# Cross-attention with a second attention branch on one core: attended values as one piece, the transposes of y as a stage of their own, and a least amount of fill for each step

## The chip, the cores and the metric

The kernel runs on one core of one Trainium2 chip. The metric is the device time of one execution in microseconds (us), here the median of several runs. The core has a matrix engine (TensorE, "PE"; its loads of stationary operands are listed apart as "PEld"), VectorE ("DVE"), ScalarE ("ACT") and GpSimd ("POOL"); SyncE ("SP") issues most of the transfers. Every engine works through its own list of instructions in the listed order, and semaphores join the lists. Matrix products are accumulated in PSUM, a memory of eight banks, and must be copied or reduced out of it by another engine before the bank can be used again.

## What is computed

The inputs are x, 2 x 2048 x 640 numbers in float32, a context of 2 x 128 x 384, and weights. The context's first 124 tokens are text tokens; its last 4 form a second branch. There are 8 heads of 80.

```python
query = hidden_states @ Wq
keyt = enc @ Wk
valt = enc @ Wv
hs = _mha(query, keyt, valt)                        # softmax over 124 keys
ca_q1 = jnp.einsum('btc,th->bch', ca, Wq_ca)        # 384 distinct rows
ca_q1 = ca_q1[:, indices, :]                        # spread over 2048 rows
ca_hs1 = _mha(ca_q1, residual, residual)            # keys and values are x itself
ca_q2 = ca_hs1 @ Wq
ca_hs2 = _mha(ca_q2, ca @ Wk_ca, ca @ Wv_ca)        # softmax over 4 keys
out = (hs + ca_hs2) @ Wout + b_out + residual
```

Since the 2048 queries of the second branch are only 384 distinct rows, that branch is computed for 384 rows and its part of the output is added to the row tiles by an indirect transfer.

## The kernel before

The 2 x 2048 rows of x are cut into 32 row tiles of 128 rows, two of which make a *unit* (16 units, m = 0 to 15), and into 8 *blocks* of 512 rows (b, sb). Two streams of work share TensorE.

**The second branch** is the main line, once per batch b. `yz_block` (L712) multiplies a block of x, transposed, with a small matrix (tiles `pyz`), ScalarE copies the result out and adds ones (L731, tile `yz`), and TensorE turns it by eight transposes (tiles `pt_y`) which are copied into `y_sb`. `maxima` (L743) computes scores `s1`, 4 matmuls of a small tile shape at a time into four banks, and VectorE takes their maxima (`mx`, 2.3 us each). `less_maxima` (L762) subtracts them. `contraction` (L776) computes the scores again the other way round (`s2`), ScalarE takes the exponential of them (`ea`, L807), and TensorE accumulates `acc` from `ea` and `y_sb`; at its end stand a transpose (`pt_acc`), small operations on VectorE (`prod`, `s2f`, `p2`), a transpose (`pt_p2`) and three products (`po2`) whose result `o2` is written to DRAM.

**The text branch** is the fill. For a unit m it consists of `queries` (tiles `pq`, five matmuls each), `scores` (L918: two `sc` tiles of three matmuls per row tile; VectorE takes the maximum `m` and subtracts it, ScalarE takes the exponential in one instruction for both), `divided` (L955: VectorE sums, `r`, and GpSimd multiplies, L962), `turned` (L965: VectorE transposes both row tiles into `eb`, one transfer writes them to DRAM as `kept`, and after `wait` further steps four transfers read them back as `pT`), and `values` (L994: three tiles `ph` of attended values, the first two of four matmuls, the third of eight with a smaller shape, each copied to `hsT`; then four tiles `po` of five matmuls for the output projection, each added to the row tile `xo` by VectorE). Row tiles that are finished before `o2` exists are written to a buffer in DRAM (`early`) and are read back (`xe`) and completed later.

**What sets the order.** All matmuls are kept in the order in which the program emits them. `TensorInOrder` (L20) adds up a planned time `pe.us` for them. `weave(main, fill)` (L1106) runs the main line step by step; each step yields a gap in planned microseconds, and `fill.run` then emits pieces of the fill until the gap is used. A piece ends where the fill's generator yields; it may overshoot the gap, and the debt, a negative `due`, is carried to the next steps, which then may get no piece at all. `Mix` (L133) takes pieces in turn from its fills: `own` (what the main line needs next: loads, transposes of x, `yz` blocks), `text` and `later`. Each part is a `Stage` with needs: names in `done` or conditions. `x_turn` (L694) needs 24 planned us after its load. `Mix.until` (L159) forces parts through up to a named one. `ahead(m)` (L1120) makes unit m's stage: `together` (L1074) runs `turned(m + 1)`, `residual(m + 1)`, `completed`, the queries and scores of unit m + 2 and `values(m)` in turn, one piece of each at a time. So between two `ph` tiles of unit m stands a piece of each of the others, a score tile `sc` for instance.

PSUM: three banks (`ps_m`), to which a fourth (`ps_a`) is added in the second batch's maxima, serve the tiles of the fill and the small ones of the main line; four banks hold `s1` or `s2`. From the end of the second contraction on, eight banks serve the fill. `evacuate` (L268) copies a tile out on VectorE in the first contraction, on ScalarE in the second batch's maxima, on both in turn in the second contraction and the tail.

The phases by the trace of before: setup to 58 us, maxima of batch 0 to 169, contraction 0 from 171 to 312, maxima of batch 1 to 482, contraction 1 from 484 to 625, the tail (units 10 to 15, without a main line) to the end.

The functions that the change touches, and what calls them:

Of the kernel before, what the change touches and what calls it, by code (L numbers as in the profile page):

```python
# [19 lines left out]
class TensorInOrder:  # L20
# [3 lines left out]
    def __init__(self, tc):  # L24
        self.tc, self.us = tc, 0.0
# [107 lines left out]
class Mix:  # L133

    def __init__(self, pe, *fills):
        self.pe, self.fills, self.at = pe, [[f, w, f.us] for f, w in fills], None

# [19 lines left out]
    def until(self, done, what):  # L159
        while what not in done:  # L160
            for f, _, _ in self.fills:
                if any(getattr(p, "what", None) == what for p in f.parts):
                    while self.at is not None and self.at is not f and self.at.open:
                        self.at.step(self.pe)
                    self.at = f
                    if not f.step(self.pe):
                        assert what in done or self.step(), what
                    break
            else:
                assert what in done, what  # L170
# [3 lines left out]
def kernel(  # L174
# [40 lines left out]
    pe = TensorInOrder(tc)  # L215
# [8 lines left out]
    NSB = S // 512  # L224
# [15 lines left out]
    done = set()  # L240
    slots = Slots(done, xqp, NSB + 1)
# [400 lines left out]
    blocks = [(b, sb) for b in range(B) for sb in range(NSB)]  # L642
    yz_of, o2_of, q_of, e_of, pT_of, xr_of, early_of = {}, {}, {}, {}, {}, {}, {}
    whole = set()
    coming = []

    def x_tile(b, sb, again):

        users = [] if again else [("yz", b, sb)]
        users += [("q", b, sb)] if again or b == 0 else []  # L650
        t = slots.tile([P, 4, NCH, P], f"xt_{b}_{sb}", users)
        for kind in ("q",) if again else ("q", "yz") if b == 0 else ("yz",):
            xt[kind, b, sb] = t
        return t
# [57 lines left out]
    def yz_block(b, sb):  # L712


        t = xt["yz", b, sb]
        yz = yz_of[b, sb] = cap.tile([P, 2, 512], F32, tag="yz", name=f"yz_{b}_{sb}", bufs=NSB + 1)
        ps = [mm_tile(f"pyz_{b}_{sb}_{u}") for u in range(2)]
        for c in range(4):
            half = slice(2 * G * (c % 2), 2 * G * (c % 2 + 1))
            matmul(  # L720
                ps[c // 2][half, :], wyz[:, b, c, :, :].rearrange("p j k -> p (j k)"), t[:, :, c, :],
                start=True, stop=False, skip_group_check=True,
            )
        for u in range(2):
            half = slice(2 * R * u, 2 * R * (u + 1))
            matmul(
                ps[u], wyz4[half, b, :, :].rearrange("p g k -> p (g k)"), t[half, :, 4, :],
                start=False, stop=True, skip_group_check=True,
            )
        for u in range(2):  # L730
            nc.scalar.activation(yz[:, u, :], ps[u], AF.Identity, bias=ones)  # L731
        yield
        for u in range(2):
            py = mm_tile(f"pt_y_{b}_{sb}_{u}")
            for k in range(4):
                transpose(py[:, k * P : (k + 1) * P], yz[:, u, k * P : (k + 1) * P], ident)
            evacuate(
                y_sb[:, 4 * sb : 4 * sb + 4, 4 * u : 4 * u + 4, :].rearrange("p s g k -> p s (g k)"),
                py.rearrange("p (s k) -> p s k", s=4),
            )  # L740
            yield
# [220 lines left out]
        nc.gpsimd.tensor_tensor(et, et, r.unsqueeze(2).to_broadcast([P, HEADS, NK]), ALU.mult)  # L962
        e_of[b, st] = e

    def turned(m, wait=3):  # L965


        eb = pools["eb"].tile([P, 4, 2, HEADS, R], F32, tag="eb", name=f"eb_{m}")
        for k, at in enumerate(tiles(m)):
            last = dve.last  # L970
            ins = dve.transpose(eb[:, :, k], e_of.pop(at).rearrange("p h (j b) -> p j h b", j=4))
            dve.behind(ins, last)
        kept = hbm.tile([P, 4, 2 * HEADS * R], F32, tag="hbm", name=f"kept_{m}")
        dma(kept, eb.rearrange("p j k h a -> p j (k h a)"))
        for _ in range(wait):
            yield
        pT = pT_of[m] = pools["pT"].tile([P, 4, 2, HEADS, R], F32, tag="pT", name=f"pT_{m}")
        by_keys = kept.rearrange("(i b) j n -> j b i n", i=4)
        for j in range(4):
            dma(pT[R * j : R * (j + 1)].rearrange("p i k h a -> p i (k h a)"), by_keys[j])  # L980
        yield
# [12 lines left out]
    def values(m):  # L994

        N = 2 * P
        b = tiles(m)[0][0]
        xr = xr_of.pop(m)
        pT = pT_of.pop(m)
        hsT = []  # L1000
        for c0, n in ((0, 2), (2, 2), (4, 1)):
            ph = mm_tile(f"ph_{m}_{c0}")
            for k in range(n):
                for h in (2 * (c0 + k), 2 * (c0 + k) + 1) if c0 < 4 else ():
                    half = slice(VH * (h % 2), VH * (h % 2 + 1))
                    matmul(
                        ph[half, k * N : (k + 1) * N], vpad[b][:, h, :VH], pT[:, :, :, h, :].rearrange("p i k a -> p k i a"),
                        start=True, stop=True, skip_group_check=True,
                    )
            for h in (0, 2, 4, 6, 1, 3, 5, 7) if c0 == 4 else ():  # L1010
                quarter = slice(R * (h // 2), R * (h // 2 + 1))
                matmul(
                    ph[quarter, :N], vpad[b][:, h, VH:], pT[:, :, :, h, :].rearrange("p i k a -> p k i a"),
                    start=(h % 2 == 0), stop=(h % 2 == 1), skip_group_check=True,
                )
            t = pools["ht"].tile([P, n * N], F32, tag=f"ht{n}", name=f"hsT_{m}_{c0}", bufs=2)
            evacuate(t, ph[:, : n * N])
            hsT += [t[:, k * N : (k + 1) * N] for k in range(n)]
            yield
        for k, (b, st) in enumerate(tiles(m)):  # L1020
            rows = slice(k * P, (k + 1) * P)
            for u in range(2):
                cols = slice(u * HALF, (u + 1) * HALF)
                po = mm_tile(f"po_{b}_{st}_{u}")
                for c in range(NCH):
                    matmul(
                        po[:, :HALF], hsT[c][:, rows], wout_sb[:, c, cols],
                        start=(c == 0), stop=(c == NCH - 1),
                    )
                    if c == 2:  # L1030
                        yield WITHIN
                dve.tensor_tensor(xr[k][:, cols], xr[k][:, cols], po[:, :HALF], ALU.add)
                yield
            if ("o2", b) in done:
                if m not in whole:
                    add_second(xr[k], b, st)
                dma(out[b, st * P : (st + 1) * P, :], xr[k])
            else:
                early_of[b, st] = hbm.tile([P, H], F32, tag="early", name=f"early_{b}_{st}", bufs=8)
                dma(early_of[b, st], xr[k])  # L1040
# [30 lines left out]
    def stage(what, gen, *needs):  # L1071
        return Stage(done, what, gen, *needs)
# [32 lines left out]

    def weave(main, fill):  # L1106

        due = 0.0
        for gap in main:
            due = fill.run(due + gap)  # L1110

    mx_of = {}
    sq_stack = ExitStack()
# [32 lines left out]
    def rows_stages(b, sb, *needs, again=False):  # L1146
        return [
            stage(("load", b, sb), x_load(b, sb, again), lambda: not coming, *needs),
            stage(
                ("again" if again else "x", b, sb), x_turn(),  # L1150
                lambda: not coming or pe.us > coming[0] + 24.0,
            ),
        ]

    def yz_stage(b, sb, *needs):
        return stage(("yz", b, sb), yz_block(b, sb), *needs)

    def early(n):
        needs = [("x", *blocks[n])] if n else []
# [3 lines left out]
    own = Fill(  # L1163
        done,
        loads[0][0],
        stage("keys", setup_keys()),
        loads[0][1],
        loads[1][0],
        yz_stage(0, 1, ("half", 0, 0)),
        loads[1][1],  # L1170
        loads[2][0],
        stage("values", setup_values()),
        yz_stage(0, 2, ("half", 0, 1)),
        loads[2][1],
        yz_stage(0, 3, ("half", 0, 2)),
    )
    text = Fill(done, *[early(n) for n in range(NSB)])
    Mix(pe, (text, 1)).run(12.5)
    fill = Mix(pe, (own, 1), (text, 1))
    weave(setup_a2(), fill)  # L1180
    own.parts.insert(0, yz_stage(0, 0))
    for sb in range(NSB):
        fill.until(done, ("yz", 0, sb))
        weave(maxima(0, sq, mx_of[0], sb, 2.4), fill)
# [12 lines left out]
        own.add(*rows_stages(1, sb, slots.free(1)))  # L1197
    later = Fill(done, *rows_stages(1, 0, slots.free(1), ("x", 1, 1), again=True))
    for sb in range(2, NSB):
        later.add(*rows_stages(1, sb, slots.free(1), ("yz", 1, 0)))  # L1200
    for sb in range(1, NSB):
        later.add(*rows_stages(1, sb, slots.free(1), ("room", NSB + sb - 1), again=True))
    fill = Mix(pe, (own, 1), (text, 1), (later, 1))
# [4 lines left out]
    on[0] = "A"  # L1208
    ps_turns[:] = [ps_m, ps_m, ps_m, ps_a]
    own.add(  # L1210
        yz_stage(1, 0),
        *[yz_stage(1, sb, ("half", 1, sb - 1), ("x", 1, sb)) for sb in range(1, NSB)],
    )
    for sb in range(NSB):
        fill.until(done, ("yz", 1, sb))
# [42 lines left out]
```

## Time and profile before

| | |
|---|---|
| median of 9 runs | 771.64 us (769.08 to 773.0) |
| profiled execution | 770.01 us, of which the span from first to last instruction is 768.3 |
| granted TensorE clock, mean | 0.998 |
| busy in the span: PE, PEld | 740.6 us, 378.9 us |
| busy in the span: DVE, ACT, POOL | 374.5 us, 195.1 us, 134.3 us |
| most costly groups on PE: po, pq (both weights), sc, s (both ways), acc, ph | 187.4, 188.0, 95.4, 114.1, 54.6, 51.1 us |

The profile gives for each engine the time in which it was busy, in the order of its groups of instructions ("out<-in", with the shapes) and the idle time just before them with the engine that ended it ("<-DVE hsT" means that the copy into hsT came last). The timeline lists instructions by start (us) and duration (us), neighbours of one kind joined into one row with "xN"; in brackets stands the idle time ahead of it. A matmul on 32-bit data is listed as two records, so a tile of three matmuls is "x6". In the text a distance is taken from start to start, which includes what a matmul's neighbours cost it.

### The profile page before, as it was taken

The page shows a single profiled execution, that of the slowest core. Times are in us where ns is not written, and L with a number is a line of the kernel's source. Part 1 is how long each engine was busy: PE and PEld are TensorE (multiplying, and loading weights), DVE is VectorE, ACT ScalarE, POOL GpSimd, SP SyncE. Part 2 cuts the span into 40 slices and gives each one's busy share as a digit, 9 for nine tenths or more (in the row PEclk, how much of TensorE's full clock was granted, in tenths as well). Part 3 has the DMA queues.
Part 4 walks back from the last instruction along what each step waited for, and adds up shares of the span by engine and source line. Part 5 has one row for each costly group of instructions (what it writes and reads, how often), then busy time and mean ns, then how long its engine had stood idle before and what let it go on. Part 6 is the DMA issues. An engine that isn't in the chain of part 4 may idle for free.

```text
span 768.3 us, 9354 instructions
## 1 busy us (share of the span) xinstructions
PE 740.6 (96%) x3785; PEld 378.9 (49%) x3785; DVE 374.5 (49%) x502; ACT 195.1 (25%) x241; POOL 134.3 (17%) x192
## 2 busy tenths in 40 slices
PE   7999999999998999989999999999999999999997
PEld 4653343343344445555545454444533556556664
DVE  2134753563365345578758586421530626346631
ACT  2212121104335433231111110443534321011100
POOL 7000000000111012217221221010010022432320
PEclk9999999999999999999999999999999999999999
DMA  9704540000476664499997267320920427785873
GB/s 287 164 0 69 71 85 0 1 0 1 131 124 139 155 121 130 131 236 197 266 185 209 52 151 130 110 52 18 181 67 1 150 71 222 163 219 168 215 216 90
DMA packets 146853, 95.63 MB, mean 124 GB/s; under 512 B 118069, under 2 KB 118389, under 8 KB 144762
## 3 DMA queue, kind: packets, MB, share of 16 engines
q1 hardware_dynamic: 141690, 84.44, 44.2%
q0 software_dynamic: 5120, 10.59, 8.0%
q8 instruction: 30, 0.49, 0.3%
q14 instruction: 13, 0.11, 0.0%
HBM read 63.48 MB, written 31.52 MB: 124 GB/s over the span
## 4 chain that ended last, share of the span: by engine, by line
PE 87%; DVE 6%; DMA 2%; ACT 2%; issue 2%; POOL 0%; SPq 0%; DVEq 0%; ACTq 0%; POOLq 0%
PE po L28 22%; PE pq L28 22%; PE s L28 13%; PE sc L28 10%; PE acc L28 6%; PE ph L28 5%; PE pyz L28 3%; DVE m L55 1%; DVE p L55 1%; PE pk L28 1%; ACT ea L807 1%; PE pt_y L41 1%; DVE mx L55 1%; PE pv L28 1%; DMA pT<-kept 1%
## 5 line engine op out<-in xcount | busy, mean ns | idle before, releaser
L28 PE MATMUL po<-wout_sb,hsT 128*128 128x320 f32 x640 | 187.4, 438 | 0.9 <-DVE xo L55 0.6
L28 PEld LDWEIGHTS po<-wout_sb,hsT 128*128 128x128 f32 x640 | 118.3, 190 | 72.0 <-issue 28.2
L55 DVE TENSOR_REDUCE mx<-s 128x4 f32<-128x2048 f32 x48 | 109.9, 2289 | 83.0 <-PE s L28 83.0
L28 PE MATMUL pq<-xt,wq_sb 128*128 128x512 f32 x320 | 150.2, 605 | 0.0
L807 ACT ACTIVATE ea<-s 128x1536 f32<-128x1536 f32 x64 | 92.7, 1448 | 105.2 <-PE s L28 105.1
L55 DVE TENSOR_TENSOR xo<-xo,po 128x320 f32<-128x320 f32 x64 | 31.0, 484 | 152.7 <-PE po L28 152.7
L962 POOL TENSOR_TENSOR p<-p,r 128x992 f32<-128x992 f32 x32 | 63.6, 2030 | 231.2 <-DVE r L55 221.6
L28 PE MATMUL sc<-kpad,q 128*128 128x248 f32 x384 | 95.4, 385 | 2.2 <-DVE p L55 1.6
L28 PEld LDWEIGHTS pq<-xt,wq_sb 128*128 128x128 f32 x320 | 57.4, 189 | 79.4 <-issue 74.7
L28 PEld LDWEIGHTS sc<-kpad,q 128*128 128x128 f32 x384 | 68.8, 189 | 32.9 <-issue 19.4
L28 PE MATMUL s<-ca,yz 32*128 32x384 f32 x512 | 59.4, 533 | 4.5 <-ACT ea L807 4.1
L268 ACT COPY q<-pq 128x512 f32<-128x512 f32 x30 | 17.6, 585 | 164.1 <-PE pq L28 164.1
L55 DVE TENSOR_REDUCE m<-sc 128x4 f32<-128x496 f32 x64 | 42.3, 663 | 34.0 <-PE sc L28 34.0
L28 PE MATMUL s<-yz,ca 32*128 32x512 f32 x384 | 54.7, 640 | 3.2 <-DVE mx L55 3.2
L1044 POOL DMA_INDIRECT xo<-o,query x25 | 39.2, 1569 | 92.3 <-DVE xo L55 23.7
L28 PE MATMUL acc<-ea,y_sb 128*32 128x384 f32 x512 | 54.6, 498 | 0.0
L28 PE MATMUL ph<-pT,vpad 128*32 128x256 f32 (+1 forms) x512 | 51.1, 387 | 2.2 <-DMA pT<-kept 1.9
L947 ACT ACTIVATE p<-p 128x992 f32<-128x992 f32 x32 | 33.0, 1031 | 74.2 <-DVE p L55 74.0
L55 DVE TENSOR_TENSOR p<-sc,m 128x496 f32<-128x496 f32 x64 | 42.7, 669 | 1.6
L268 ACT COPY hsT<-ph 128x512 f32<-128x512 f32 (+1 forms) x25 | 12.9, 515 | 106.3 <-PE ph L28 106.2
L55 DVE STREAM_TRANSPOSE eb<-p 128x1024 f32<-128x1024 f32 x32 | 38.0, 1222 | 2.2 <-POOL p L962 2.2
L55 DVE TENSOR_REDUCE r<-p 128x8 f32<-128x992 f32 (+1 forms) x34 | 37.9, 1115 | 0.0
(136 smaller groups left out, 435.8 us busy)
## 6 DMA issues: line engine op xcount, KB each, us to landing
kept<-eb SPq DMA_DIRECT2D x16, 1024.0 KB, 4.8
pT<-kept SPq DMA_DIRECT2D x64, 256.0 KB, 5.1
xi<-in_x_dram SPq DMA_DIRECT2D x44, 256.0 KB, 6.4
xo<-in_x_dram SPq DMA_DIRECT2D x32, 320.0 KB, 5.1
out_dram<-xo SPq DMA_DIRECT2D x25, 320.0 KB, 2.7
xi<-in_x_dram SPq DMA_DIRECT2D x44, 64.0 KB, 5.2
early<-xo SPq DMA_DIRECT2D x7, 320.0 KB, 2.2
xe<-early SPq DMA_DIRECT2D x7, 320.0 KB, 5.1
```

The source lines that it names most:

```text
L28: ins = self.tc.nc.tensor.matmul(out, lhsT, rhs, **kw)
L41: ins = self.tc.nc.tensor.transpose(out, in_, ident)
L55: self.last = getattr(self.tc.nc.vector, name)(*args, **kw).ins
L268: nc.scalar.copy(dst, src)
L807: nc.scalar.activation(e, q4[:, :, :CAD], AF.Exp, scale=SCALE)
L947: nc.scalar.activation(e[:, :, :NK], e[:, :, :NK], AF.Exp, scale=SCALE)
L962: nc.gpsimd.tensor_tensor(et, et, r.unsqueeze(2).to_broadcast([P, HEADS, NK]), ALU.mult)
L1044: nc.gpsimd.indirect_dma_start(out=t, out_offset=None, in_=o2_of[b], in_offset=bass.IndirectOffsetOnAxis(ap=query[:, st : st + 1], axis=0) ...
```

## The change

1. `values`: the `yield` behind each of the three `ph` tiles becomes a single one behind all three. The sixteen matmuls of a unit's attended values are one piece.
2. `turned`: the transfers of `pT` are issued after two further steps instead of three.
3. The `yz` stage becomes two: `yzT` (the matmuls `pyz` and ScalarE's copies) and `yz` (the transposes `pt_y` and their copies), which needs a planned time of 1.0 us since the first. The slot of the transposed x is free, and later loads may start, with `yzT`.
4. `weave`: what a step may fill is at least 0.5 planned us (or the step's own gap, where that is less), whatever the debt. So each step with a gap gets at least one piece.
5. `Mix.until` sets `Mix.hurry` where nothing else is left to step; two conditions on planned time are then passed over.

```diff
@@ class Mix
+    hurry = False
@@ Mix.until
-                    if not f.step(self.pe):
-                        assert what in done or self.step(), what
+                    if not f.step(self.pe) and what not in done and not self.step():
+                        Mix.hurry = True
+                        assert f.step(self.pe), what
+                        Mix.hurry = False
@@ x_tile
-        users = [] if again else [("yz", b, sb)]
+        users = [] if again else [("yzT", b, sb)]
@@ yz_block
             nc.scalar.activation(yz[:, u, :], ps[u], AF.Identity, bias=ones)
+        yz_at[b, sb] = pe.us
         yield
+
+    def y_rows(b, sb):
+
+        yz = yz_of[b, sb]
         for u in range(2):
             py = mm_tile(f"pt_y_{b}_{sb}_{u}")
@@ turned
-    def turned(m, wait=3):
+    def turned(m, wait=2):
@@ values
             hsT += [t[:, k * N : (k + 1) * N] for k in range(n)]
-            yield
+        yield
@@ weave
-            due = fill.run(due + gap)
+            due = fill.run(max(due + gap, min(gap, 0.5)))
@@ rows_stages
-                lambda: not coming or pe.us > coming[0] + 24.0,
+                lambda: Mix.hurry or not coming or pe.us > coming[0] + 24.0,
@@ yz_stage
-    def yz_stage(b, sb, *needs):
-        return stage(("yz", b, sb), yz_block(b, sb), *needs)
+    def yz_stages(b, sb, *needs):
+        return [
+            stage(("yzT", b, sb), yz_block(b, sb), *needs),
+            stage(("yz", b, sb), y_rows(b, sb), lambda: Mix.hurry or pe.us > yz_at[b, sb] + 1.0),
+        ]
@@ the loads of later blocks
-        later.add(*rows_stages(1, sb, slots.free(1), ("yz", 1, 0)))
+        later.add(*rows_stages(1, sb, slots.free(1), ("yzT", 1, 0)))
```

The calls of `yz_stage` become calls of `yz_stages`, whose two parts stand one behind the other in the same places. The transposes and matmuls, their shapes and their numbers are those of before. In the order that results, the three `ph` tiles of a unit are adjacent in all sixteen units (before, in units 14 and 15), ten row tiles go through `early` instead of seven, and in one tile of queries and one of attended values ScalarE and VectorE exchange their parts as copiers.

## The prediction

> **What bounds the kernel now.** I read the page first, then TensorE's waits, then stretches of the timeline, then the clock by windows.
>
> ```profile
> PE 740.6 (96%) x3785; PEld 378.9 (49%) x3785; DVE 374.5 (49%) x502; ACT 195.1 (25%) x241; POOL 134.3 (17%) x192
> PE 87%; DVE 6%; DMA 2%; ACT 2%; issue 2%; POOL 0%; SPq 0%; DVEq 0%; ACTq 0%; POOLq 0%
> ```
>
> TensorE (PE) is busy for 96% of the span and is 87% of the chain that ended last. The change issues the same matmuls in another order, so it can only save in two places: in TensorE's waits, and in what a matmul costs after a neighbour of another shape. The waits by releaser (us in total, times, longest):
>
> ```profile
> PE s L28 <- ACT ea L807: 4.1, 5, 1.8
> PE s L28 <- DVE mx L55: 3.2, 3, 1.4
> PE pt_y L41 <- ACT yz L731: 3.1, 4, 0.8
> PE ph L28 <- DMA pT<-kept: 1.9, 1, 1.9
> PE sc L28 <- DVE p L55: 1.6, 1, 1.6
> ```
>
> These five are 13.9 us. The timeline of unit 0 in contraction 0 shows how such a wait arises:
>
> ```profile
> 222.60 3.65 POOL L962 TENSOR_TENSOR p<-p,r 128x992 f32<-128x992 f32 x2 [21.60 <-DVE r L55]
> 226.28 1.25 DVE L55 STREAM_TRANSPOSE eb<-p 128x1024 f32<-128x1024 f32 x1 [0.56 <-POOL p L962]
> 227.44 0.64 DVE L55 TENSOR_REDUCE m<-sc 128x4 f32<-128x496 f32 x1
> 228.00 0.68 DVE L55 COPY hsT<-ph 128x512 f32<-128x512 f32 x1
> 228.74 1.08 PE L28 MATMUL ph<-pT,vpad 128*64 128x256 f32 x8 [0.23 <-DVE hsT L55]
> 233.07 0.93 PE L28 MATMUL s<-ca,yz 32*128 32x384 f32 x8 [1.79 <-ACT ea L807]
> ```
>
> VectorE works in order: it waits for GpSimd's product, transposes it (eb), and only then reduces scores that stood ready since 222.7 and copies out ph_0_0. TensorE meanwhile had other work, 6.05 us between ph_0_0 (222.69) and ph_0_2 (228.74), so it paid 0.23. That other work is what the change takes from between the ph tiles.
>
> **The change, part by part.** The sum is made against the profiled execution: 770.01 us, of which 768.3 span. The median of the nine runs, 771.64, lies 1.63 above it; I add a difference to the median.
>
> *Order alone.* The program's counts of matmuls are equal. (a) Three ph tiles with other work between them cost 1.01 each (ph at 222.69, next matmul 223.70); the one group that before already has together (750.36 to the po at 753.24) costs 2.88. 14 of 16 units are split before: 14 x (3.04 - 2.88) = 2.1 to 2.2 saved. (b) Two sc tiles between small-tile matmuls cost 2.70 together (216.89 to 219.59), one alone 1.46 (213.79 to 215.25): a pair of switches between full-array and small-tile matmuls is 0.22, about 0.1 each. The order after has 29 switches fewer (259 to 230): 2.8. (c) acc followed directly by a ph of the last chunk is cheaper by 0.11 than elsewhere; four such places go: +0.45; pt_y beside other neighbours +0.15. Sum -4.3.
>
> *Waits that go.* pt_y behind ACT's yz costs 0.84 over its usual distance at four places (0.77 idle in the row); the split puts other work there at three, the first has nothing to take: -2.5. In contraction 0 and around unit 3 the distances exceed the usual ones by 0.30, 1.87, 0.43, 1.33, 0.52, 0.14, 0.75 and 1.72 (227.65 to 333.6; the rows 233.07 and the sc wait of 1.6 are among them): -7.1. Three later ones, 0.75, 0.34, 0.39: -1.5. Sum -11.1. The s waits behind mx at 79.5 and 140.7 stay (same neighbours in both orders), the startup stays, and so does the wait of ph_15 for its transfer: eb_15 moves by 0.05 against it, 1.9 becomes 1.9 to 2.1. So -15.4 in all.
>
> *New stall, unit 0.* Contraction 0 turns over three PSUM banks, and the third ph tile gets the bank of the first: it waits for the copy hsT_0_0, which stands behind both eb transposes and the reduce. Before: sc_0_3_1 starts at 218.25 (second of the pair at 216.89), its copy hsT_0_0 ends at 228.68, 10.43 later, and that chain (reduce, subtract, Exp, sum, product, transposes) is the same after. By the matmul prices ph_0_4 comes 6.42 after sc_0_3_1. Stall 10.49 - 6.42 = **4.1**.
>
> *New stall, unit 3.* Its VectorE queue, as before runs it:
>
> ```profile
> 310.10 1.18 DVE L55 TENSOR_REDUCE r<-p 128x8 f32<-128x992 f32 x1
> 311.71 3.03 DVE L55 STREAM_TRANSPOSE xt<-xi 128x512 f32<-128x512 f32 x5
> 314.66 1.15 DVE L55 TENSOR_REDUCE r<-p 128x8 f32<-128x992 f32 x1
> 315.72 0.48 DVE L55 TENSOR_TENSOR xo<-xo,po 128x320 f32<-128x320 f32 x1
> 316.46 1.84 POOL L962 TENSOR_TENSOR p<-p,r 128x992 f32<-128x992 f32 x1 [2.32 <-DVE r L55]
> ```
>
> From the first row to the end of GpSimd's product are 8.2 us; after adds three small operations (0.5), the transpose of that product (1.25) and the subtract (0.66) that frees sc_0_10_0's bank: 10.7. The first row comes 4.55 after pt_acc (s2f 1.48 after it, the row 3.07 later), so the bank is free 15.25 after pt_acc. ph_3_4, which takes that bank, stands 10.2 after pt_acc by the matmul prices; before it had 23 us between the two scores, after 6.6. Stall **5.1**, 2.0 of it before ph_3_2 (behind the xo add) and 3.1 before ph_3_4; 0.25 more at the po that follows.
>
> *Exp behind Exp.* ACT is in order too. Where the second sc of a tile stands directly before an s of the contraction, Exp of the scores goes ahead of Exp ea, and the next s comes no earlier than 5.33 after that sc (183.39 to 188.72, 0.43 waited). Seven new places, 0.45 each and a little: 3.3. Units 10 and 4 lose 0.45 and 0.2 by the subtract behind eb. All new stalls: 4.1 + 5.1 + 0.25 + 3.3 + 0.65 = **13.4**.
>
> *The clock.*
>
> ```profile
> 49.30:52.70 3.40, 2.09 (x17) 1.72 (x16) 1.48 (x7) 0.75 (x2) 0.00 (x0) 0.98 0.00 0
> 52.70:56.10 3.40, 3.21 (x8) 0.86 (x8) 3.40 (x11) 0.00 (x0) 0.00 (x0) 0.52 0.01 2
> 229.70:233.10 3.40, 1.61 (x12) 1.09 (x10) 2.76 (x5) 2.37 (x2) 0.00 (x0) 1.00 0.95 280
> ```
>
> (Columns: length, then busy time of PE, PEld, DVE, ACT, POOL, then PEclk.) After 3.4 us in which TensorE was busy for 2.09, the clock was 0.52 for 3.4 us and two pairs of pyz took 1.73 and 1.66 instead of 0.91 and 0.96: 1.5 lost. A stretch busy for 1.61 with one idle piece of 1.79 (last row) kept its clock, as did one with 1.93 idle at 748.4. Idle pieces of 4.1 and of 5.1 with 0.9 of work inside are in no row: each costs 0 to 1.5. Both are more than twice the longest that was harmless, so I take 1.5 each: **+3.0**, ends 0 and 3.0. [...]
>
> *Cover that gets thin.* Along the same steps units 1, 2, 7, 8, 9 and 10 hold, with 0.8, 0.65, 0.2, 0.45, 0.5 and 0.6 us to spare, 3.2 in sum. Nothing in the trace says that a step may not be late by so much; ends 0 and 3.2, I take half: **+1.6**. (They could not gain: a bank that is free earlier starts nothing earlier.)
>
> *Moved issues.* The four pT transfers of a unit are issued one step earlier on SP, and three more row tiles go through the early buffer (3 writes, 3 reads, 320 KB each; 0.34 us of SP per write in the rows). SP's queue is shared with the xi loads, whose six issues took 10.27 from 323.86; the pT of units 3, 4 and 5 still land before their ph. Nothing, as long as they do; a pT behind such a load would cost up to 10. Three indirect adds on GpSimd (1.57 each) move later, behind no product that TensorE waits for. One copy of q goes to ACT's side in exchange for one hsT on VectorE: 0.1, hidden.
>
> Sum: -15.4 + 13.4 + 3.0 + 1.6 = **+2.6**: 772.6 in the profiled execution, **774.2** against the median. About 0.2% (1.5 us) is what a measurement of this kernel can tell from no change.
>
> **Rivals.**
> *A: the stalls come, the clock and the thin covers hold.* For it: the harmless 1.79 and 1.93. Then -15.4 + 13.4 = -2.0: 769.6.
> *B, the other side: faster, since the two long stalls do not come.* Its place is VectorE's queue at units 0 and 3: if the reduce and the subtract of the next scores, or the copy of ph, were done while VectorE waits for GpSimd's product, the banks would be free in time and with the stalls (9.2) the clock's 3.0 would go. Then 2.6 - 12.2 = -9.6: 762.0, and 760.4 where the thin covers hold. It decides once 4.2 of those 12.2 are absent. For it: TensorE's distance is only short at two units of 16. Against it: the rows at 226.28 to 228.00, where ready scores waited behind eb.
> *C: slower by more.* The three copies of a unit's ph now come at once, on VectorE and ACT, each 0.68 and one 0.43; where a reduce or a subtract stands behind them, the next sc waits up to 1.8 less the 1.3 of that sc's own length. At the eight units with three banks 0.5 each is 4, with the thin covers in full (1.6 more): 774.2 + 5.6 = 779.8. Against it: in the walk the next sc takes a bank that is not the last copied.
> *D: the change doesn't do what it says.* The order does change (ph tiles are adjacent in all 16 units), so this is only the case in which gains and losses meet: part of A and of the forecast.
>
> **How the numbers follow.** Forecast 0.44 (own range 771 to 777; 0.34 slower, 0.10 within the bound), A 0.20 (0.12 faster, 0.08 within), B 0.18 (faster), C 0.18 (slower). Faster 0.30, same 0.18, slower 0.52. The range goes from B with thin covers lost to C and a little more: 762 to 781; B's own lower half and what lies beyond C are left out.
>
> **What would show it.** In TensorE's waits of the changed kernel: pt_y behind yz once, 0.8; the sc wait of 1.6 gone; a ph wait for DVE of about 4 near 220 us and a pair of 2 and 3 near 322 to 326; s behind ACT ea about seven times 0.4; ph behind pT still near 2. The clock by windows right after both ph waits: near 0.5 if the forecast is right, 1.0 under A. No ph wait over 1 us means B and proves the walk along VectorE's queue wrong; many waits of sc or po behind hsT mean C. I am also wrong if pT arrives late in a unit, which would be a ph wait on DMA in the middle of the span.

## The result, and the profile after

The changed kernel takes 777.5 us (median of 20 runs, 773.32 to 781.57); the kernel before, run beside it, 772.76 (62 runs). The ratio is 1.0061, with a 95% interval of 1.0042 to 1.008: slower by 4.7 us, between 3.2 and 6.2. The profiled execution has a span of 771.6 us against 768.3, and a mean granted clock of 0.989 against 0.998. Both are among the quickest of their kernels: over the executions on record the mean granted clock goes from 0.981 to 0.989 with the change and from 0.988 to 0.998 without it, so the profiles show what happens where, and the medians what it costs.

The two lines of the page of after, TensorE's share of busy time and the chain that ended last:

```profile
PE 739.8 (96%) x3785; PEld 383.2 (50%) x3785; DVE 378.0 (49%) x502; ACT 194.4 (25%) x241; POOL 133.7 (17%) x192
PE 86%; DVE 6%; issue 2%; ACT 2%; DMA 2%; POOL 1%; SPq 0%; DVEq 0%; ACTq 0%; POOLq 0%
```

By these two lines nothing happened: the bound and its share are those of before. TensorE's waits in after, by what ended them (total us, times, longest), show what did:

```profile
PE s L28 <- ACT ea L817: 4.1, 9, 0.5
PE ph L28 <- DVE hsT L55: 4.1, 1, 4.1
PE ph L28 <- DVE xo L55: 3.5, 1, 3.5
PE s L28 <- DVE mx L55: 3.2, 3, 1.4
PE ph L28 <- DVE p L55: 2.9, 1, 2.9
PE ph L28 <- DMA pT<-kept: 1.8, 1, 1.8
PE pt_y L41 <- ACT yz L736: 0.8, 1, 0.8
```

The pt_y waits went from four to one, the sc wait of 1.6 and the s wait of 1.8 are gone, as the change has it. In their place stand three waits of ph, 10.5 us in all, and more but shorter s waits behind ACT ea (nine of at most 0.5). The first ph wait is at unit 0 (timeline of after, start and duration in us, the wait in brackets):

```profile
217.14 3.64 POOL L972 TENSOR_TENSOR p<-p,r 128x992 f32<-128x992 f32 x2 [13.60 <-DVE r L55]
220.82 1.25 DVE L55 STREAM_TRANSPOSE eb<-p 128x1024 f32<-128x1024 f32 x1 [0.56 <-POOL p L972]
221.99 0.64 DVE L55 TENSOR_REDUCE m<-sc 128x4 f32<-128x496 f32 x1
222.55 0.67 DVE L55 COPY hsT<-ph 128x512 f32<-128x512 f32 x1
223.28 1.93 PE L28 MATMUL ph<-pT,vpad 128*32 128x256 f32 x16 [4.06 <-DVE hsT L55]
```

The order on VectorE is that of before, row for row; TensorE has come to it 4.1 us too early, since the work that stood between the ph tiles is now behind them. The other two are at unit 3:

```profile
319.95 1.84 POOL L972 TENSOR_TENSOR p<-p,r 128x992 f32<-128x992 f32 x1 [5.67 <-DVE r L55]
320.07 1.84 DVE L55 TENSOR_TENSOR p2pad<-p,r 128x96 f32<-128x96 f32 x1
321.83 3.07 DVE L55 STREAM_TRANSPOSE xt<-xi 128x512 f32<-128x512 f32 x5
325.90 0.47 DVE L55 TENSOR_TENSOR xo<-xo,po 128x320 f32<-128x320 f32 x1
326.42 1.08 PE L28 MATMUL ph<-pT,vpad 128*64 128x256 f32 x8 [3.50 <-DVE xo L55]
328.50 1.25 DVE L55 STREAM_TRANSPOSE eb<-p 128x1024 f32<-128x1024 f32 x1 [0.33 <-POOL p L972]
329.67 0.64 DVE L55 TENSOR_TENSOR p<-sc,m 128x496 f32<-128x496 f32 x1
330.45 1.94 PE L28 MATMUL ph<-pT,vpad 128*32 128x256 f32 x16 [2.95 <-DVE p L55]
```

One row is new in kind: p2pad, a product of 96 numbers per partition, took 1.84 us where before's in the same batch took 0.25, and it ended 0.12 after GpSimd's product beside it. The clock by windows (length, busy PE, PEld, DVE, ACT, POOL, then PEclk) behind the first wait:

```profile
220.00:222.00 2.00, 0.00 (x0) 0.00 (x0) 1.45 (x3) 0.00 (x0) 0.85 (x2) 1.00 0.97 154
222.00:224.00 2.00, 0.72 (x8) 0.40 (x12) 2.00 (x5) 0.00 (x0) 0.12 (x1) 0.60 1.02 153
224.00:226.00 2.00, 2.00 (x20) 0.71 (x12) 0.82 (x2) 0.00 (x0) 0.00 (x0) 0.50 1.02 355
226.00:228.00 2.00, 2.00 (x16) 0.20 (x8) 0.00 (x0) 1.07 (x1) 0.00 (x0) 0.50 0.96 332
228.00:230.00 2.00, 2.00 (x10) 1.44 (x6) 0.00 (x0) 0.38 (x1) 0.00 (x0) 0.70 0.50 197
```

A mean of 0.60 is half speed for 0.8 of the 2 us from 222 to 224; with the 4 us that follow and 0.6 of the last 2 that is 6.8 us of half speed. Unit 3 has the same, 328.2 to 335.

Distances from start to start can be added up against the usual distance of the same matmuls, as the prediction did. The last matmul starts at 757.25 us before and at 760.82 after: the order saves 4.3; waits of before that went, the startup's included, 12.8; the three stalls cost 4.1, 3.7 and 3.05; seven new s waits behind Exp 0.56 each, 3.9; units 10 and 12 and a po 1.0; the half clock 2.8 at unit 0 and 2.2 at unit 3. That is -17.1 + 20.7 = +3.6, which is the difference of the two starts.

### The profile page after: what moved, and what is told of

It is laid out like the page before. It is cut to its first block, busy times and chain, and to the rows that moved or that the text cites. A ratio compares the mean times of both kernels' runs of the same rounds, so it can differ in the third digit from the quotient of the medians.

```text
span 771.6 us, 9362 instructions
## 1 busy us (share of the span) xinstructions
PE 739.8 (96%) x3785; PEld 383.2 (50%) x3785; DVE 378.0 (49%) x502; ACT 194.4 (25%) x241; POOL 133.7 (17%) x192
## 4 chain that ended last, share of the span: by engine, by line
PE 86%; DVE 6%; issue 2%; ACT 2%; DMA 2%; POOL 1%; SPq 0%; DVEq 0%; ACTq 0%; POOLq 0%
PE pq L28 22%; PE po L28 20%; PE s L28 13%; PE sc L28 11%; PE acc L28 6%; PE ph L28 5%; PE pyz L28 3%; ACT ea L817 2%; DVE m L55 1%; DVE p L55 1%; PE pk L28 1%; PE pv L28 1%; DVE mx L55 1%; DMA pT<-kept 1%; PE pt_y L41 1%
## 5 line engine op out<-in xcount | busy, mean ns | idle before, releaser
L28 PE MATMUL po<-wout_sb,hsT 128*128 128x320 f32 x640 | 189.8, 440 | 0.5 <-DVE p L55 0.5
L972 POOL TENSOR_TENSOR p<-p,r 128x992 f32<-128x992 f32 x32 | 59.3, 1881 | 272.7 <-DVE r L55 272.7
L28 PEld LDWEIGHTS sc<-kpad,q 128*128 128x128 f32 x384 | 72.0, 193 | 28.3 <-issue 13.1
L28 PE MATMUL ph<-pT,vpad 128*32 128x256 f32 (+1 forms) x512 | 49.3, 401 | 12.3 <-DVE hsT L55 4.1
L1054 POOL DMA_INDIRECT xo<-o,query x22 | 34.4, 1564 | 99.5 <-DMA xo<-in_x_dram 43.8
L28 PEld LDWEIGHTS ph<-pT,vpad 128*32 128x32 f32 (+1 forms) x512 | 24.2, 126 | 34.9 <-issue 13.6
```

Source lines behind the costliest of these rows:

```text
L28: ins = self.tc.nc.tensor.matmul(out, lhsT, rhs, **kw)
L1054: nc.gpsimd.indirect_dma_start(out=t, out_offset=None, in_=o2_of[b], in_offset=bass.IndirectOffsetOnAxis(ap=query[:, st : st + 1], axis=0) ...
```

## Experiments

All ratios are to the kernel before on the same chip, with 95% intervals. The theory: the change is a gain except for two places where VectorE's queue can't free a bank in time; the stalls there, and the clock behind them, cost more than everything else saves. The rival: the grouping of ph costs in every unit.

**1. Is the clock a consequence of the stall, and what is it worth?** The changed kernel, in `values`, ahead of the tiles that waited:

```diff
+            busy = {(0, 4): 4, (3, 2): 3, (3, 4): 3}.get((m, c0), 0)
+            if busy:
+                us = pe.us
+                idle = sq.tile([P, 4, 512], F32, tag="sq", name=f"idle_{m}_{c0}")
+                for k in range(busy):
+                    matmul(idle[:, k, :], ident, wout_sb[:, 0, :512], start=True, stop=True)
+                pe.us = us
             ph = mm_tile(f"ph_{m}_{c0}")
```

> The changed kernel, with matmuls on data that nobody reads (their product goes to a free score bank) put where TensorE stood idle: four in unit 0 ahead of the third ph tile, three ahead of the second and three ahead of the third in unit 3, 0.86 us each. Every wait and every other instruction stays. Theory (the long stalls also lower the clock): the ph waits shrink to under 1 us each since TensorE is at work in them, ph starts no earlier than in the changed kernel, the clock stays 1.0 after both places, and the 5.0 us that the half clock cost (2.8 at unit 0, 2.2 at unit 3, by distances against the usual ones) go: 1.000 of before, where the changed kernel is 1.006. Rival (the clock fell for another reason, on its own period, or its cost is hidden): the clock still goes to 0.5 near 223 and 328 us and the time stays at 1.006.

Measured: 772.88 us, 0.9997 (0.9965 to 1.0029); waits of ph 0.7 and 0.4. The windows of that kernel around units 0 and 3:

```profile
218.00:228.00 10.00, 9.57 (x66) 4.34 (x63) 8.60 (x12) 2.37 (x2) 3.84 (x4) 1.00 1.12 152
228.00:238.00 10.00, 9.52 (x65) 4.48 (x66) 1.80 (x4) 5.27 (x4) 0.00 (x0) 1.00 0.91 255
320.00:330.00 10.00, 9.28 (x38) 4.81 (x37) 9.63 (x17) 0.04 (x1) 3.75 (x3) 1.00 0.08 33
330.00:340.00 10.00, 9.55 (x48) 5.72 (x47) 4.62 (x8) 3.09 (x6) 0.49 (x3) 1.00 0.59 205
```

The clock is 1.00 at both places (in the setup it is at half for two stretches, so the mean is 0.996). ph_0_4 still comes 4.13 later than its usual distance, and yet the kernel is some 5 us faster than the changed one, by the two ratios. Ten matmuls more make it faster: of the 15.9 us that the stalls cost in the profile (10.9 of waiting, 5.0 of clock) a third is the clock that they leave behind.

**2. Undo the grouping at units 0 and 3 alone.**

```diff
-        yield
+            if m in (0, 3) or c0 == 4:
+                yield
```

> The changed kernel with the yield behind each ph tile put back in units 0 and 3 alone. Theory (the loss is the long stalls at these two units and the clock behind them): the ph waits of 4.1, 3.5 and 2.9 go, the mean clock is back at 0.998; 10.9 of stalls and 5.0 of clock go, 0.9 comes back for ten more switches of shape and some 4.7 for such waits as before had at these units: 10.3 us less than the changed kernel, 767 us, 0.993 of before. Rival (what costs is the grouping of ph as such, in all units): over 1.003 of before.

Measured: 774.84 us, 1.0026 (0.9993 to 1.006). Better than the changed kernel, but not 0.993. The ph waits over 2 us are gone; in that kernel's list of TensorE's waits stands instead:

```profile
PE po L28 <- DVE p L55: 4.4, 2, 3.9
PE ph L28 <- DVE hsT L55: 1.8, 1, 1.8
```

The 3.9 ends at 325 us, in unit 3, at the small po2 matmuls, which now come where the ph tiles were and wait for the same subtract (p); the clock is at half from 322.0 to 328.8. So the stall at unit 3 isn't made by the grouping of its ph tiles. It goes with the distance: the next unit's first score follows the last one of the unit before after 6.6 us, where the kernel before has 20.8 by the prices, and VectorE can't be through by then, whatever stands in line for the bank. My expectation had taken a cause for one thing that was two.

**3. The grouping alone,** in the kernel before (the yield moved out of the loop, nothing else).

> The kernel before with nothing but the three ph tiles made one piece. Theory: by the price of the order 5.7 us less than before; unit 0 has the same short distance from the last score to the third ph (6.3 us where 10.5 are needed), so one stall of 4.2 and 2.8 of clock, in exchange for 2.2 of waits that before had there; unit 3's distance is 15 us for the score and 18 for ph where the changed kernel has 6.6 and 9.9, so no stall there. Sum -0.9, with the other waits of before in contraction 0 (4.9 in all) staying or going: 767 to 772, 0.994 to 0.999 of before. Rival (the grouping alone makes both stalls, and the other parts nothing): 1.005 of before with ph waits of 4 near 220 and 3 to 6 near 325.

Measured: 776.24 us, 1.0033 (0.9999 to 1.0066). The ph wait of 4.1 at unit 0 is there, with one stretch of half clock of 3.4 us behind it (some 1.5 lost), and no ph wait at unit 3. The estimate of 0.994 to 0.999 was too good, and the trace doesn't say in full why. It has smaller waits that the estimate left out, but those behind ScalarE (acc 0.85, pt_acc 0.65, s 0.94 and less) stand in the trace of run 4 too, which came out as expected. Run 3's own is a po that waits 1.98 behind xo, up to 330.9; the same wait is 0.58 in run 4.

**4. The grouping in all units but unit 0,** in the kernel before (the condition is `m == 0 or c0 == 4`).

> The kernel before with the three ph tiles made one piece in all units but unit 0. Theory: the order is 5.5 us cheaper, no stall over 2 us, clock 0.998; the waits that before had at unit 0 (2.2) stay: 767 us, 0.993 of before, and less if waits in the rest of contraction 0 go. It would beat both kernels. Rival (the grouped ph tiles starve VectorE or ACT in units other than 0): 0.999 or more, with waits on hsT or p spread over the units.

Measured: 768.61 us, 0.9934 (0.9905 to 0.9962), as expected. The edit differs from run 3's at unit 0 alone: the stall there, with its clock and the longer po wait that follows in unit 3, goes with a loss of 0.3% where without it there is a gain of 0.7%. The rival, that grouping costs in all units, is out.

**5 and 6. The other two parts alone,** in the kernel before: the yz stage made two, and the line of `weave`.

> The kernel before with nothing but the yz stage made two. Theory (each part alone is a gain or nothing, the loss comes with the grouping of ph): order -0.1 us, the waits of pt_y behind yz go from four to one or two, -1.7 to -2.5, no ph, po or sc wait over 2.5 us, clock 0.998: 0.995 to 0.999 of before. Rival (the two-part stage is what brings the next unit's score close behind the last one at unit 3, 13.9 us by prices where before has 20.8, and so the stall there): a wait of 3 or more near 325 us, clock under 0.995, 1.002 or more.

> The kernel before with nothing but the least fill of 0.5 for each step. Theory: order +0.3 us; the s waits behind ACT's Exp (4.1 in before, 1.8 the longest) shrink to some 0.5 each, at most -2.5; unit 3's score comes 15.7 after the last one and ph 17 to 27 after, enough for its bank: no new stall. 0.996 to 1.000 of before. Rival (fill in each step crowds the scores and is the source of a stall): 1.002 or more, with a ph, sc or po wait over 3.

Measured: 769.18 us, 0.9943 (0.9911 to 0.9975), and 769.69 us, 0.9957 (0.9932 to 0.9981). Both are gains, in the ranges expected or a little better. Where run 6 gains is not where it was expected: the s wait of 1.8 stands as in before, and what is gone is the sc wait of 1.6. The run with yz alone has a half clock all the same, at 325 to 332 us, behind a single idle piece of 1.84 at unit 3's first ph (its timeline, then its windows):

```profile
324.79 1.40 PE L28 MATMUL ph<-pT,vpad 128*64 128x256 f32 x8 [1.84 <-issue]
```

```profile
325.00:328.00 3.00, 3.00 (x12) 1.65 (x9) 0.69 (x1) 0.00 (x0) 0.00 (x0) 0.57 0.94 266
328.00:331.00 3.00, 3.00 (x8) 1.91 (x6) 0.00 (x0) 0.75 (x2) 0.00 (x0) 0.50 0.98 372
```

**7. VectorE beside GpSimd.** The changed kernel, with one product moved:

```diff
-        dve.tensor_tensor(
+        nc.gpsimd.tensor_tensor(
             p2pad[:, :, n2 : n2 + HEADS * T]...
```

> The changed kernel with the small product p2pad, which took 1.84 us on VectorE while GpSimd's product p ran beside it (0.25 in before, where nothing ran), issued on GpSimd behind that product. Theory (VectorE's product of two SBUF operands stood still for GpSimd's): VectorE's five transposes start 1.7 us earlier, the ph wait behind xo goes from 3.5 to 1.8, the one behind p stays at 2.9; p2pad is done near 322, in time for its transposes. 1.7 us less than the changed kernel, 1.004 of before, more if the clock recovers sooner. Rival (the 1.84 is a record's error or the stall has another end): waits 3.5 and 2.9 as they were, 1.006.

Measured: 775.43 us, 1.0034 (1.0003 to 1.0064). Its timeline at unit 3:

```profile
322.95 1.84 POOL L972 TENSOR_TENSOR p<-p,r 128x992 f32<-128x992 f32 x1 [5.65 <-DVE r L55]
322.95 3.04 DVE L55 STREAM_TRANSPOSE xt<-xi 128x512 f32<-128x512 f32 x5
324.76 0.35 POOL L856 TENSOR_TENSOR p2pad<-p,r 128x96 f32<-128x96 f32 x1
327.51 1.08 PE L28 MATMUL ph<-pT,vpad 128*64 128x256 f32 x8 [1.58 <-DVE xo L55]
```

The transposes run beside GpSimd's product without delay, and the wait behind xo falls from 3.5 to 1.6. The half clock behind the stalls lasts 3.4 us there instead of 6.8. So the 1.84 was real, and it was on the path. By the intervals the time alone doesn't tell this kernel from the changed one; the waits do.

**8. A version from the parts that gain:** the kernel before with ph as one piece in all units but unit 0, and the yz stage made two in batch 1 alone; `wait=3` and the line of `weave` as before.

```diff
@@ values
+            if m == 0 or c0 == 4:
+                yield
@@ yz_stages (`both` runs the two parts as the one stage of before)
+        if (b, sb) in ((0, 0), (0, 1), (0, 2), (0, 3)):
+            return [stage(("yz", b, sb), both(b, sb), *needs)]
```

> The kernel before with ph as one piece in all units but unit 0, and with the yz stage made two in batch 1 alone; wait and fill as before. Unit 3's score then comes 12.9 and ph 16.4 to 18.3 after the last score, about as in the kernel with ph one piece but in unit 0 (15.0; 16.5 to 18.4), which was 0.9934 of before. Theory: three pt_y waits of 0.84 and a wait of s behind mx of 0.63 go, nothing new comes: 3 us less than that kernel, 765.5 us, 0.990 of before. Rival (at unit 3, or in the maxima of batch 1, the saved waits come back at another place): 0.993 or more.

Measured: 765.76 us, 0.9886 (0.985 to 0.9923). It beats both kernels: by 1.1% the one before, by 1.7% the changed one.

**9. The cause at unit 0.** The changed kernel, with another engine for three copies and the matmuls in the same order:

```diff
-            evacuate(t, ph[:, : n * N])
+            if m == 0:
+                nc.scalar.copy(t, ph[:, : n * N])
+            else:
+                evacuate(t, ph[:, : n * N])
```

> The changed kernel with the three ph tiles of unit 0 copied out by ScalarE in place of VectorE; the order of the matmuls is the same to the last. The bank of the third ph tile and the one of the score after it then wait for ScalarE, which is free there, and no longer for a queue in which GpSimd's product and two transposes stand first. Theory: the ph wait of 4.1 and the half clock behind it (2.8) go, the unit 3 stall stays: 6.9 us less than the changed kernel, 0.997 of before. Rival (the third ph tile waits for something else, or the score after it inherits the wait): a wait of 2 or more within 10 us of it, 1.001 or more.

Measured: 770.6 us, 0.9959 (0.9929 to 0.9988), 1.0% under the changed kernel for three copies. Timeline of that kernel:

```profile
216.94 2.30 PE L28 MATMUL ph<-pT,vpad 128*64 128x256 f32 x20
218.07 0.59 ACT L1028 COPY hsT<-ph 128x512 f32<-128x512 f32 x1 [0.27 <-PE ph L28]
218.69 1.25 DVE L55 STREAM_TRANSPOSE eb<-p 128x1024 f32<-128x1024 f32 x1 [0.74 <-POOL p L972]
```

ScalarE copies before VectorE has begun its first transpose, and ph goes on without a break. So the grouping needs no stall at unit 0: it makes the distance short, and the copy's place in VectorE's queue makes the stall. At unit 3 this kernel still waits 3.5 and 2.1.

**10. Both remedies together:** the version of run 8 with ph as one piece in every unit, unit 0's copied by ScalarE.

> The kernel before with ph as one piece in every unit, unit 0's copied out by ScalarE, and the yz stage made two in batch 1 alone. Theory: against the kernel with unit 0 left split (0.9886 of before) the two waits at unit 0 (0.30 and 1.86) and 0.43 behind them go, the order is 0.2 cheaper, and one new s wait behind Exp of 0.5 comes: 2 us less, 763.7 us, 0.986 of before. Rival (VectorE's queue at unit 0 delays a later score or po by as much): 0.988 or more.

Measured: 766.76 us, 0.9912 (0.9878 to 0.9946). The waits at unit 0 are gone, but a po waits 1.99 behind xo, up to 321.3, where run 8 has 0.58, and the clock is at half for 3.4 us behind it. The rival holds: no better than run 8, and by the intervals not told apart from it.

**11. The changed kernel without the division of the yz stage.**

> The changed kernel without the division of the yz stage: ph as one piece, least fill, wait 2. Theory (the unit 3 stall comes from the parts together, which crowd the next unit's score and ph behind the last score: 15.0 to ph by prices with ph alone, less with each part more): score 8.0 and third ph 12.3 after the last score, where the changed kernel has 6.6 and 9.9 and ph in fact came 16.6 after it. So at unit 3 a stall of 2.5 to 4.3 with half clock behind it in place of 6.7; unit 0 as in the changed kernel (4.1 and 2.8); pt_y waits back at four (+2.5). 1.002 to 1.007 of before. Rival (one part alone, the division, makes the unit 3 stall): no wait over 1.5 near 325 us and 1.000 or less.

Measured: 779.56 us, 1.009 (1.0052 to 1.0128). The rival is out: the unit 3 stall is smaller (2.2, and one stretch of half clock) but there, without the division. New is an s wait of 3.0 behind mx at 368.8 us, which left the clock at 1.00, and the pt_y waits are back: worse than expected, though by the intervals not told apart from the changed kernel.

**12. The changed kernel with `wait=3`.**

> The changed kernel with the pT transfers issued after three further steps, as before; the matmuls stand in the same order to the last. Theory: nothing on the chain changes, the transfers land in time either way; same stalls of 4.1, 3.5 and 2.9, 1.005 to 1.007 of before. Rival (the earlier issue hides a transfer or holds up SP's queue): a ph wait for DMA in the middle of the span, or one less at the end, and 2 us or more of difference.

Measured: 782.83 us, 1.0132 (1.0079 to 1.0184). The theory is out, the rival holds. At unit 1, in a timeline of TensorE:

```profile
266.42 1.97 PE L28 MATMUL ph<-pT,vpad 128*64 128x256 f32 x8 [5.69 <-DMA pT<-kept]
```

With the same order of matmuls, pT is issued a step later and lands too late, and the clock falls in that wait too: its mean is 0.57 from 264 to 272 us. The grouping alone doesn't bring this: runs 3, 4 and 8 group ph, keep `wait=3` and have no such wait. In the changed kernel's order as a whole ph comes too early after its transposes for `wait=3`, and the shorter wait is what pays for that.

## Why the prediction was right, and where it wasn't

The forecast was slower by 2.6 us, 774.2 on a median of 771.64. Measured is slower by 4.7 us, 777.5 on a median of 772.76. (777.5 itself lies just above the forecast's own range of 771 to 777; 4.7 on its median of 771.64 is 776.3, inside it.) The likeliest case occurred, in its places and by its waits. That the total came this near is in part luck, since terms that were too low and too high cancel below.

- *Order alone, -4.3:* not measured by itself, but the sum of the result closes with it. (29 switches at 0.11 each are 3.2, where the prediction wrote 2.8.)
- *Waits that go, -11.1:* all listed ones are gone. The sum is 12.8 by the trace; 0.8 of the rest is the startup, whose first pyz starts at 52.12 instead of 52.89 after the same matmuls.
- *Stall at unit 0, 4.1:* measured 4.06 idle, 4.12 by distance, for hsT_0_0 behind the transposes. Run 9 shows the cause: the copy's place in VectorE's queue.
- *Stall at unit 3, 5.1 (2.0 behind xo and 3.1 behind p):* measured 6.7 (3.7 and 3.05). The first term was mis-sized by 1.6, since I priced p2pad at 0.25 within "three small operations (0.5)". A row of before told against that, and I had passed it by; see the last section. In run 7, with p2pad off VectorE, that wait is 1.58 instead of 3.50.
- *Exp behind Exp, 3.3:* seven places, as listed, 0.56 each: 3.9.
- *The clock, +3.0:* measured 5.0 in the profiled execution. Both stalls did bring it down. The step took one stretch of 3.4 us for each, as in the one row of before; there were two of them in a row for each. How many come is no matter of the stall alone: behind the same wait of 4.1 at unit 0 runs 3, 11 and 12 have one. Run 1 shows that the idle is the cause at these places and that it is worth about this much. (The prediction says that no row of before has an idle piece of 4; its start has one of 4.17, with a granted clock of 1.00, but nothing ran ahead of it.)
- *Cover that gets thin, +1.6:* measured 0.2 (a ph of unit 12). The walk was more exact than half of its margins. Against the trace's +3.6 the terms stand thus: unit 3, Exp and clock together 4.2 too low, cover 1.4 too high, the waits that go 1.7 too low. The last 1.1, from +3.6 to the medians' +4.7, lies within the interval of the result.
- *Moved issues, nothing:* right for the changed kernel as it is, 1.8 at the end and none in the middle. That the step between is worth some 5.5 us by the two ratios (run 12) I had not seen: I named 10 us as the price of a late pT, and not that the shorter wait is what keeps it from being paid.

The rivals: A (stalls without the clock) is what run 1 built, 772.9, and it did not come by itself. B (no long stalls) is run 8's and run 9's world. It needs another engine for the copy or another order; VectorE did not step out of order. C (grouped copies starve VectorE in all units) is out by runs 4 and 8. D did not arise.

In the changed kernel the clock fell 3.2 us into the idle piece of 4.06 at unit 0, and 0.7 us into the second of the two pieces at unit 3 (3.5 and 2.95). Over all runs the length of an idle piece doesn't tell whether the half clock comes: 1.84 in run 5 and 1.99 in run 10 had it behind them too, while 1.93 in before, 2.4 at the end of run 1's kernel and 3.01 in run 11 had not.

What the three parts do alone, 0.9943, 0.9957 and 1.0033, would give 0.993 together, and the changed kernel has 1.0061. Some 9 us of the difference of 10 can be put down to the stall at unit 3 with its clock (6.7 and 2.2). None of the three has it alone, though yz alone has 1.84 of idle and 6.8 us of half clock there and ph alone a po wait of 1.98: by the prices of the order the next unit's score comes 20.8 us after the last one in before, 15.0 with ph alone, 13.9 with yz alone, 15.7 with the fill alone, and 6.6 with all of them; runs 2 and 11 show the stall with one of them weakened or gone. The fourth, `wait=2`, was not run alone, and this account stays an argument from prices.

## What to carry to other kernels

Work between two users of a bank is cover, so before such pieces are joined, follow the queue of the engine that frees the bank from the last thing that it waits for, and compare that time with the distance that is left; where it is short, move one copy to a free engine, as run 9 did, before the order is given up. A stall on TensorE may cost more than its length: here the half clock behind 10.9 us of waits cost another 5.0, while a wait of 3.0 in run 11 had none behind it. Each part of a change that tightens an order is to be tried alone and together, since margins are used up by the sum.

## What the runs showed of the hardware

VectorE's product p2pad, of two operands in SBUF, issued beside GpSimd's product, ended 0.12 us after that product at unit 3 of after and in batch 1 of before. The pair in the kernel before, which the prediction passed over:

```profile
615.97 1.84 POOL L962 TENSOR_TENSOR p<-p,r 128x992 f32<-128x992 f32 x1 [14.46 <-DVE r L55]
617.01 0.92 DVE L55 TENSOR_TENSOR p2pad<-p,r 128x96 f32<-128x96 f32 x1
```

GpSimd ends at 617.81 and VectorE at 617.93; in after they end at 321.79 and 321.91. With no product of GpSimd's beside it, p2pad took 0.25 (before, at 309.94) and 0.21 (after, at 636.09). VectorE's transposes, which read one operand, ran beside the same product at their usual length (3.04 against 3.03 for five, run 7). Why the one was held up and the others were not, these traces do not show.

The half clock came in stretches of about 3.4 us, one (before, run 7 at unit 3, run 3 at unit 0), two in a row (after, at both places) or three (run 9 at unit 3, 10 us by its windows), and it went on while TensorE was fully busy again (after, 224 to 228 us: busy for 4.00 of 4.00 us at a clock of 0.50).

In after these stretches start at 51.72, 222.39 and 328.20, which are 50 and 31 times 3.413 us from one to the next; in run 7, by its windows, at 54.8, 225.4 and 331.3, the same multiples; in run 12, of those that its windows place, at 55.9 and 407.4, 103 times.

What decides whether an idle piece brings the half clock stays open. In nine of the fourteen profiled executions (runs 1, 3, 4, 5, 7, 8, 10, 11 and 12) it also came in the setup, where TensorE was busy for all 16.00 us from 16 to 32: the mean clock from 24 to 32 us is 0.57 to 0.89 there. In the other five TensorE was as busy, and the clock was 1.00.
